# Halo copies issued by SyncE, the last minimum and maximum of a convolution moved behind a norm's sums, and a first pair of tiles normalised in halves

## Chip, cores and metric

The kernel runs on one core of a Trainium2 chip. The metric is the device time of one execution in microseconds; lower is better. An execution of the kernel before takes 2997.45 us (median of three, 2994.02 to 2998.33).

## What is computed

The input x has the shape (T, B, N, D) = (4, 8, 512, 512) in float32. Four layers follow each other, each of the form x = x + L(groupnorm(x)), with four groups of two channels for each t:

```
x = x + L0(gn(x))   # spiking attention block, by far the longest part
x = x + L1(gn(x))   # depthwise 13x13 Gaussian convolution, reflected edges
x = x + L2(gn(x))   # quantised 3x3 convolution, 8 channels to 8
x = x + L3(gn(x))   # 3x3 convolution with a bias

# L2:
sx  = 127 / max(abs(gn(x)))             # one maximum over the whole tensor
qx  = clip(round(gn(x) * sx), -127, 127)
out = conv3x3(qx, qw) / (sx * sw) + bias
```

Two things in this matter here. The scale of layer 2 needs the largest |gn(x)| of the whole tensor, so layer 2 can't start before layer 1 has given its last element. And the norm of layer 3 at time t needs all of layer 2's result of that t.

## The kernel before

Layer 0 ends a little after 2100 us and is not touched. Layer 1 and the fused layers 2 and 3 follow.

**Layer 1.** `Layer1.image` (from line 779) convolves one image on TensorE (PE, L797). For each half `a` of it, ScalarE evicts the result (L804), VectorE (DVE) takes its statistics (`bn_stats`, L806), its maximum `hi` (L807) and its minimum `lo` (L808), and DMAs on ScalarE's and GpSimd's queues (L815) write it to HBM. After the last image of a pair of channels, `next_norm` (from line 840) forms the group's mean and standard deviation: `group_stats` sums over the free axis on DVE (L175, `gsum_x`), sums over the partitions with a small matmul (L178, `gps_x`), squares the differences and sums again, and GpSimd (POOL) takes the power -0.5 (L195, `grstd_x`). `group_steps` is the same as a generator, which hands control back after the sums and after the matmul. From mean, deviation, `hi` and `lo` comes the largest |gn(x)| of the group (L854 to L858); `layers23` (from line 979) takes the maximum over the groups and partitions (L989 to L1001) and folds the scale into `r_own` and `mr_own` (L1009, L1010).

**Layers 2 and 3.** The rows of one t lie in tiles of 128 partitions (windows of rows times channels) by 512 columns. Two tiles make a pair, 22 pairs one t (N_PAIRS), the last with only half a tile. The loop at the end of `layers23` runs over n = 0 to 112. Each step has:

- a load of a pair (SyncE, L1033), five pairs ahead;
- `normalise`, two pairs ahead: two copies x to u on POOL that reorder columns (L1047), then y = u * r + mr on ScalarE (ACT, L1051, 128 x 1024 in one instruction);
- `quantise`, one pair ahead: xq, rounded to bfloat16, on DVE (L1062, 128 x 1024 in one instruction);
- `layer2`: three bfloat16 matmuls for each of the two tiles (L1080), and for each tile an instruction on DVE that adds u and writes layer 2's result into the ring x3 (L1087, called x in the profile), with its statistics by ACT (a square, L1093) or DVE (`bn_stats`, L1098);
- some halo copies (L1236). Layer 3 reads for each window also the row above and below, which lie in another window's partitions. `halos` gives the small copies within x3, from SBUF to SBUF. Every 11 pairs, from n = 14 on, a new list is made and worked off one or two copies per step. All in all there are 50 DMAs, issued by POOL;
- from n = 25 on `layer3` of pair n - 25: POOL writes the edge columns (L1175), 24 matmuls (L1182), two evictions o on ACT (L1191) and two stores on SyncE (L1198);
- behind the last pair of a t, `norm3`, a generator of which two steps run in each turn of the loop. It forms layer 3's norm (L1133 to L1164) and scales the weights `band_t` with it (L1151).

PSUM has three buffers for layer 2 and four for layer 3; u has four buffers, y two, o ten.

**What sets the order.** An engine works off its instructions in the order in which they stand in the program. That order is not wholly the one of the Python code: a planner lays it down when the program is built, from dependencies and estimated times. `tc.issue_after(op)` keeps an instruction behind another one: in each step `normalise` and `quantise` stand behind layer 2's instructions of the step before, and `layer2` behind these and behind layer 3 of the step before. On PE layer 2 and layer 3 alternate by pairs.

Of the kernel before, what the change touches and what calls it, by code (L numbers as in the profile page):

```python
# [37 lines left out]
AF = mybir.ActivationFunctionType  # L38
ALU = mybir.AluOpType
AX = mybir.AxisListType  # L40
# [3 lines left out]
T, B, N, D, H = 4, 8, 512, 512, 8  # L44
DH = D // H
NC = N // P
G = 4
# [3 lines left out]
ROUND = 12582912.0  # L51
# [9 lines left out]
N_PS1 = 4  # L61
# [65 lines left out]
def network(ctx: ExitStack, tc: tile.TileContext, i: dict, out: bass.AP):  # L127
    nc = tc.nc
# [3 lines left out]
    x2d = [tc.dram_tile([N * B, D], F32, name=f"x2_{t}") for t in range(T)]  # L132
# [7 lines left out]
    at = 0  # L140
# [102 lines left out]
    with ExitStack() as s:  # L243
        ps_1 = s.enter_context(pool("ps_2", space=PSUM))
        layer1 = Layer1(
            s, tc, x1d, x2d, avg, group_stats, r1, mr1, st2, m2, r2, most, w_sum, head, ps_1, pool
        )
        layer1.group(0)
        for g in range(1, G):
            if g == 1:  # L250
                with ExitStack() as behind:
                    for op in layer1.started:
                        behind.enter_context(tc.issue_after(op))
                    norm1(G - 1, ps_1)
                    w23 = weights23(tc, i, late, early["y"], ps_1, ident)
            layer1.group(g)
        layer1.next_norm(G - 1)
# [505 lines left out]

class Layer1:
    def __init__(
        self, s, tc, x1d, x2d, avg, group_stats, r1, mr1, st2, m2, r2, most, w_sum, head, ps_1, pool
    ):
        nc = tc.nc
        self.__dict__.update(
            nc=nc, x1d=x1d, x2d=x2d, avg=avg, group_stats=group_stats, r1=r1, mr1=mr1, st2=st2, m2=m2,  # L770
            r2=r2, most=most, ps_1=ps_1, w_sum=w_sum,
        )
        self.band, self.eye, *self.head = head
        self.ps_c = s.enter_context(pool("ps_c", 4, space=PSUM))
        self.xp = s.enter_context(pool("x1", 3))
        self.bp = s.enter_context(pool("bt1", 2))
        self.op = s.enter_context(pool("o1", 2))
        self.ends = {}

    def image(self, g, b, t, off):  # L780
        nc = self.nc
        n_half = W1_N // 2
        hi, lo = self.ends[g]
        if (b, t) == (0, 0):
            xt, bt = self.head
        else:
            xt = self.xp.tile([K1_P, W1_N, X1_U], F32, tag="x", name=f"x1_{b}_{t}")
            load_image(nc, xt, self.x1d[t][b])
            bt = self.bp.tile([K1_P, SHIFTS, M1], F32, tag="bt", name=f"bt_{b}_{t}")
            image_bands(nc, bt, self.band, b, self.r1[:, g, t : t + 1], self.eye)  # L790
        xo = self.op.tile([P, n_half // N_PS1, N_PS1 * NV], F32, tag="xo", name=f"xo1_{b}_{t}")
        for a in range(n_half // N_PS1):
            ps = self.ps_c.tile([P, N_PS1 * NV], F32, tag="conv", name="ps_conv1")
            for z in range(SHIFTS):
                for q in range(2):
                    w0 = q * n_half + a * N_PS1
                    mm = nc.tensor.matmul(  # L797
                        ps[q * M1 : (q + 1) * M1, :],
                        lhsT=bt[:, z, :],
                        rhs=xt[:, w0 : w0 + N_PS1, z : z + NV],  # L800
                        start=z == 0,
                        stop=z == SHIFTS - 1,
                    )
            nc.scalar.activation(xo[:, a, :], ps, AF.Identity, bias=off[:, t : t + 1])  # L804
            at = b % PAIR
            nc.vector.bn_stats(self.st2[:, t, b, a, :], xo[:, a, :])  # L806
            nc.vector.tensor_reduce(hi[:, t, at, a : a + 1], xo[:, a, :], AX.X, ALU.max)  # L807
            op = nc.vector.tensor_reduce(lo[:, t, at, a : a + 1], xo[:, a, :], AX.X, ALU.min)  # L808
        if (b, t) == (0, 0):
            self.started = mm.ins, op.ins  # L810
        dst = self.x2d[t]
        for q in range(2):
            for f in range(PH):
                engine = nc.gpsimd if f % 2 else nc.scalar
                engine.dma_start(  # L815
                    bass.AP(
                        dst.tensor, dst.offset + (q * n_half * W1_OUT * B + b) * D + f * NV,
                        [[B * D, W1_OUT], [W1_OUT * B * D, n_half], [1, NV]],
                    ),
                    xo[q * M1 + f : (q + 1) * M1 : PH, :, :].rearrange("p a (w v) -> p (a w) v", v=NV),  # L820
                )
# [18 lines left out]
    def next_norm(self, g):  # L840

        nc = self.nc
        n_a = W1_N // 2 // N_PS1
        m, r = self.group_stats(
            self.st2[:, :, g * PAIR : (g + 1) * PAIR].rearrange(
                "p t b k (h z) -> p t (b k h) z", z=3
            ),
            T, PAIR * n_a * 2, None, self.avg, self.ps_1, f"x2_{g}",
        )
        nc.vector.tensor_copy(self.m2[:, :, g], m)  # L850
        nc.vector.tensor_copy(self.r2[:, :, g], r)
        every = [P, T, PAIR * n_a]
        hi, lo = (x.rearrange("p t b a -> p t (b a)") for x in self.ends.pop(g))
        nc.vector.tensor_sub(hi, hi, m.unsqueeze(2).to_broadcast(every))  # L854
        nc.vector.tensor_sub(lo, m.unsqueeze(2).to_broadcast(every), lo)
        nc.vector.tensor_tensor(hi, hi, lo, op=ALU.max)
        nc.vector.tensor_mul(hi, hi, r.unsqueeze(2).to_broadcast(every))
        nc.vector.tensor_reduce(self.most[:, g : g + 1], hi, AX.XY, ALU.max)  # L858
# [118 lines left out]
def layers23(  # L977
# [47 lines left out]
    def load(t, p):  # L1025
# [3 lines left out]
        for a, q in first.items():  # L1029
# [8 lines left out]
                ),  # L1038
            )

    def normalise(t, p):
        n, n_p = len(tiles(p)), HALF * len(windows(tiles(p)[-1]))
        x = ahead.pop((t, p))[:n_p, :n, :]
        u = early["u"].tile([P, 2, D], F32, tag="u", name="u2")
        y = early["y"].tile([P, 2, D], F32, tag="y", name="y2")
        for j in range(n):
            nc.gpsimd.tensor_copy(  # L1047
                u[:n_p, j, :].rearrange("p (v g) -> p v g", g=PH),
                x[:, j, :].rearrange("p (g v) -> p v g", g=PH),
            )  # L1050
        op = nc.scalar.activation(  # L1051
            y[:n_p, :n, :], u[:n_p, :n, :], AF.Identity, bias=w["mr"][:n_p, t : t + 1],
            scale=w["r"][:n_p, t : t + 1],
        )
        ready[t, p] = u, y[:n_p, :n, :]
        return op.ins

    def quantise(t, p):
        u, y = ready[t, p]
        n_p, n, _ = y.shape  # L1060
        xq = w["xq"][(t * N_PAIRS + p) % 3]
        op = nc.vector.tensor_scalar(  # L1062
            xq[:n_p, :n, 2 : D + 2], y, ROUND, ROUND, op0=ALU.add, op1=ALU.subtract
        )
        ready[t, p] = u, xq
        return op.ins

# [142 lines left out]
    for n in range(n_all + N_PAIRS + LAG):  # L1210
        if n < n_all:
            for m in range(6) if n == 0 else [n + 5]:
                if m < n_all:
                    load(*divmod(m, N_PAIRS))


            with ExitStack() as order:
                for op in done.values():
                    order.enter_context(tc.issue_after(op))
                for m in range(3) if n == 0 else [n + 2]:  # L1220
                    if m < n_all:
                        first = normalise(*divmod(m, N_PAIRS))
                for m in range(2) if n == 0 else [n + 1]:
                    if m < n_all:
                        then = quantise(*divmod(m, N_PAIRS))
            with ExitStack() as order:
                for op in (first, then, *behind):
                    order.enter_context(tc.issue_after(op))
                did = layer2(*divmod(n, N_PAIRS))
        next(norm, None)  # L1230
        if n_chunk < n <= n_all + 3 and n % n_chunk == 3:
            t, p = divmod(n - 3 - n_chunk, N_PAIRS)
            copies = list(halos(t, p, p + n_chunk))
            at_once = -(-len(copies) // (n_chunk - 2))
        for _ in range(min(at_once, len(copies))):
            nc.gpsimd.dma_start(*copies.pop(0))  # L1236
        if n >= N_PAIRS + LAG:
            t, p = divmod(n - N_PAIRS - LAG, N_PAIRS)
            with tc.issue_after(did):
                behind = (layer3(t, p, *norms[t]),)  # L1240
        if n < n_all and n % N_PAIRS == N_PAIRS - 1:
            norm = norm3(n // N_PAIRS)
        next(norm, None)
# [36 lines left out]
```

## Time and profile before

The page describes one execution of 2991.6 us. An engine's share is its busy time over that span.

| Engine | busy us | share |
|---|---|---|
| PE (matmul) | 2900.4 | 97% |
| DVE | 2243.8 | 75% |
| POOL | 1035.6 | 35% |
| ACT | 550.0 | 18% |

The stages that the diff touches, from the trace:

| Stage | us from the start |
|---|---|
| layer 1's last matmul ends | 2560.94 |
| layer 2's first matmul | 2573.18 |
| layer 2 alone | 2573 to 2650 |
| first matmul of layer 3 | 2650.81 |
| layers 2 and 3 together | 2651 to about 2925 |
| layer 3 alone | to about 2984 |
| end, after the last eviction and store | 2991.6 |

In a timeline line the first number is the start in us, the second the duration, then engine, line, operation, output<-input with shapes, and the number of instructions taken together. Square brackets hold the engine's idle time before it and what ended that. In a row of a table by stage the stretch and its length come first, then busy us of PE, PE's weight loads, DVE, ACT and POOL with the number of instructions in brackets, then PE's granted clock, the DMA engines' share and GB/s.

In the group of lines for the halo copies, busy time stands first, then the mean of one in ns, then POOL's idle time before them with what ended it:

```profile
L1236 POOL DMA_DIRECT2D x<-x x50 | 30.8, 618 | 18.7 <-DVE sums L1136 12.0 <-issue 2.8 <-DMA out<-o 2.8
```

The 50 issues are busy for 30.8 us on POOL in all, 618 ns each.

### The profile page before, as it was taken

Reading aid. Unit: us, or ns where it says so; the run is one execution under the profiler, and the core shown is the slowest. Engines: PE = TensorE matmul, PEld = TensorE weight load, DVE = VectorE, ACT = ScalarE, POOL = GpSimd, SP = SyncE. Lnnn points to the kernel's source line nnn. Section 1 sums busy time; section 2 is a strip of 40 time slices with the busy share of each in tenths; the row PEclk is TensorE's granted clock in tenths of the full one; section 3 lists DMA queues with packets and bytes.
Section 4 is the critical chain, followed back from the end, with each engine's and each line's share of the span. In section 5 each row is a group of like instructions: output and inputs, shape, how many; then the busy total and the mean of one; then the engine's idle time right before and its main releaser. Section 6 shows DMA issues by size and latency. Waiting matters only on the chain. (4 is left out here: it accounts for less than half of the span.)

```text
span 2991.6 us, 37579 instructions
## 1 busy us (share of the span) xinstructions
PE 2900.4 (97%) x13343; PEld 1391.5 (47%) x13377; DVE 2243.8 (75%) x3883; ACT 550.0 (18%) x859; POOL 1035.6 (35%) x1928
## 2 busy tenths in 40 slices
PE   7999999999999999999999999999999999689999
PEld 3545555555555555555555555555333333223334
DVE  7887788788769868967986886786665566888880
ACT  2200010011010001001000100100111121676674
POOL 3332233333224333323432333341211112676650
PEclk9999999999999999999999999999999999889999
DMA  5312222222222221212221111111877778698865
GB/s 189 109 58 65 78 65 65 65 64 65 78 65 65 65 72 58 78 65 65 65 69 47 58 43 51 51 56 45 208 203 216 204 210 227 160 198 223 220 175 147
DMA packets 274651, 322.16 MB, mean 108 GB/s; under 512 B 21495, under 2 KB 171711, under 8 KB 274351
## 3 DMA queue, kind: packets, MB, share of 16 engines
q1 hardware_dynamic: 212304, 236.70, 29.3%
q0 software_dynamic: 20192, 56.83, 6.1%
q10 hardware_dynamic: 41967, 26.23, 3.0%
q8 instruction: 105, 1.72, 0.3%
q14 instruction: 83, 0.68, 0.1%
HBM read 210.57 MB, written 103.60 MB: 105 GB/s over the span
## 5 line engine op out<-in xcount | busy, mean ns | idle before, releaser
L485 PE MATMUL ps_in<-w_v,xn 128*128 128x512 f32 x1024 | 465.0, 603 | 2.6 <-DVE w_kq L344 2.6
L485 PE MATMUL ps_in<-xn,w_kq 128*128 128x512 f32 x1024 | 452.9, 595 | 5.1 <-DVE v_q L441 3.7
L485 PE MATMUL ps_in<-w_kq,xn 128*128 128x512 f32 x1024 | 449.8, 592 | 0.7 <-DVE v_k L450 0.7
L797 PE MATMUL ps_conv<-x,bt 112*64 112x512 f32 x2048 | 445.1, 592 | 0.1
L521 PE MATMUL ps_b<-toep,vtok 128*64 128x512 bf16 x3072 | 373.6, 383 | 0.0
L433 ACT ACTIVATE h_q<-v_q,c_half 128x512 f32<-128x512 f32 x96 | 69.3, 722 | 1550.6 <-DVE v_q L429 1164.1
L570 POOL COPY x1s<-x1s 128x2 f32<-128x2 f32 (+1 forms) x1024 | 227.4, 276 | 297.8 <-DVE x1s L559 297.8
L548 PE MATMUL ps_out<-wp,so 128*128 128x512 f32 x1024 | 308.5, 443 | 0.0
L458 POOL TENSOR_TENSOR h_v<-h_v,c_v 128x512 f32<-128x512 f32 x96 | 123.2, 1283 | 517.1 <-DVE h_v L457 505.4
L485 PEld LDWEIGHTS ps_in<-xn,w_kq 128*128 128x128 f32 x1024 | 191.9, 190 | 228.1 <-issue 212.4
L485 PEld LDWEIGHTS ps_in<-w_kq,xn 128*128 128x128 f32 x1024 | 194.2, 190 | 222.0 <-issue 205.2
L485 PEld LDWEIGHTS ps_in<-w_v,xn 128*128 128x128 f32 x1024 | 191.6, 192 | 216.9 <-issue 211.5
L797 PEld LDWEIGHTS ps_conv<-x,bt 112*64 112x64 f32 x2048 | 146.1, 135 | 288.4 <-issue 286.7
L521 PEld LDWEIGHTS <-vtok 128*64 128x64 bf16 x3072 | 207.6, 111 | 126.2 <-issue 4.9
L1182 PE MATMUL ps_conv<-x,band_t 64*64 64x512 f32 x2040 | 246.4, 599 | 3.1 <-DVE band_t L1151 3.1
L1047 POOL COPY u<-x 128x512 f32<-128x512 f32 (+1 forms) x172 | 208.7, 1247 | 95.8 <-issue 48.5
L548 PEld LDWEIGHTS ps_out<-wp,so 128*128 128x128 f32 x1024 | 192.5, 188 | 94.6 <-issue 57.8
L559 DVE SCALAR_TENSOR_TENSOR x1s<-v_p,xr 128x256 f32<-128x256 f32 x256 | 187.0, 770 | 14.9 <-DMA x<-x1s 3.9
L195 POOL TENSOR_TENSOR grstd_x<-grstd_x,neg_half 128x1 f32<-128x1 f32 (+1 forms) x28 | 20.9, 748 | 474.0 <-DVE grstd_x L194 474.0
L815 POOL DMA_DIRECT2D x<-xo x128 | 71.4, 565 | 312.5 <-ACT xo L804 298.2
L804 ACT ACTIVATE xo<-ps_conv,off 128x512 f32<-128x512 f32 x128 | 87.7, 687 | 430.6 <-PE ps_conv L797 316.0
L458 POOL TENSOR_TENSOR h_k<-h_k,c_k 128x512 f32<-128x512 f32 x96 | 122.8, 1279 | 116.4 <-DVE h_k L457 116.4
(191 smaller groups left out, 3557.8 us busy)
## 6 DMA issues: line engine op xcount, KB each, us to landing
x<-x SPq DMA_DIRECT2D x64, 917.0 KB
x<-x SPq DMA_DIRECT2D x168, 256.0 KB
x<-x1s POOLq DMA_DIRECT2D x128, 262.0 KB, 2.5
x<-in_x SPq DMA_DIRECT2D x128, 256.0 KB
xr<-in_x SPq DMA_DIRECT2D x128, 256.0 KB
out<-o SPq DMA_DIRECT2D x164, 192.0 KB
xs<-in_x SPq DMA_DIRECT2D x112, 256.0 KB
x<-xo ACTq DMA_DIRECT2D x128, 128.0 KB
```

The costliest lines, as they stand in the source:

```text
L433: nc.scalar.activation(h, v, AF.Identity, bias=c_col, scale=0.5)
L458: nc.gpsimd.tensor_add(h, h, c_twice[n])
L485: mm = nc.tensor.matmul(ps, lhsT=lhsT, rhs=rhs, start=k == 0, stop=k == NC - 1)
L521: nc.tensor.matmul(pb[two * DH : (two + 1) * DH, :], lhsT=v[:, c, h * DH : (h + 1) * DH], rhs=toep[z][:, h, u : u + N], start=c == 0 and z ...
L548: nc.tensor.matmul(ps, lhsT=so[:, k, c * P : (c + 1) * P], rhs=wpT[z][:, k, :], start=k == 0 and z == 0, stop=k == NC - 1 and z == 1,)
L559: nc.vector.scalar_tensor_tensor(own, v.rearrange("p (g v) -> p g v", g=PH)[:, two, :], 1.0, by_phase[:, two, :], op0=ALU.is_ge, op1=ALU.add,)
L570: nc.gpsimd.tensor_copy(x1[:, f, u : u + n], x1[:, fm, um - n + 1 : um + 1][:, ::-1])
L797: mm = nc.tensor.matmul(ps[q * M1 : (q + 1) * M1, :], lhsT=bt[:, z, :], rhs=xt[:, w0 : w0 + N_PS1, z : z + NV], start=z == 0, stop=z == SH ...
L804: nc.scalar.activation(xo[:, a, :], ps, AF.Identity, bias=off[:, t : t + 1])
L815: engine.dma_start(bass.AP(dst.tensor, dst.offset + (q * n_half * W1_OUT * B + b) * D + f * NV, [[B * D, W1_OUT], [W1_OUT * B * D, n_half] ...
L1047: nc.gpsimd.tensor_copy(u[:n_p, j, :].rearrange("p (v g) -> p v g", g=PH), x[:, j, :].rearrange("p (g v) -> p v g", g=PH),)
L1182: mm = nc.tensor.matmul(ps[j][b * HALF : (b + 1) * HALF, :], lhsT=band[half, b, dx, :], rhs=x3[half, s0 + j, dx : dx + D], start=dx == 0, ...
```

## The change

Three edits, for two places in which PE isn't full: the step from layer 1 to layer 2, and the stretch with layer 2 alone.

1. The halo copies are issued by SyncE instead of POOL. This takes them out of the queue in which the copies to u stand.
2. The maximum and the minimum of layer 1's very last tile are issued inside the norm's steps, behind the first sum, so that the norm's chain needn't wait for them. For that `Layer1` gets the generator `group_steps`.
3. The first pair of layer 2 (t = 0, p = 0) is normalised and quantised tile by tile, so that the first matmuls need only the first half.

```diff
@@ Layer1.image
             nc.vector.bn_stats(self.st2[:, t, b, a, :], xo[:, a, :])
-            nc.vector.tensor_reduce(hi[:, t, at, a : a + 1], xo[:, a, :], AX.X, ALU.max)
-            op = nc.vector.tensor_reduce(lo[:, t, at, a : a + 1], xo[:, a, :], AX.X, ALU.min)
+            for end, op in ((hi, ALU.max), (lo, ALU.min)):
+                args = end[:, t, at, a : a + 1], xo[:, a, :], AX.X, op
+                if (b, t, a) == (B - 1, T - 1, n_half // N_PS1 - 1):
+                    self.last_ends.append(args)
+                else:
+                    op = nc.vector.tensor_reduce(*args)
@@ Layer1.next_norm
-        m, r = self.group_stats(
+        steps = self.group_steps(
...
+        while True:
+            try:
+                next(steps)
+                if g == G - 1 and self.last_ends:
+                    nc.vector.tensor_reduce(*self.last_ends.pop(0))
+                next(steps)
+            except StopIteration as end:
+                m, r = end.value
+                break
@@ layers23
+    def tiles_apart(t, p, n):
+
+        return [slice(j, j + 1) for j in range(n)] if (t, p) == (0, 0) else [slice(0, n)]
@@ normalise
-        op = nc.scalar.activation(
-            y[:n_p, :n, :], u[:n_p, :n, :], AF.Identity, bias=w["mr"][:n_p, t : t + 1],
-            scale=w["r"][:n_p, t : t + 1],
-        )
+        for j in tiles_apart(t, p, n):
+            op = nc.scalar.activation(
+                y[:n_p, j, :], u[:n_p, j, :], AF.Identity, bias=w["mr"][:n_p, t : t + 1],
+                scale=w["r"][:n_p, t : t + 1],
+            )
@@ quantise
-        op = nc.vector.tensor_scalar(
-            xq[:n_p, :n, 2 : D + 2], y, ROUND, ROUND, op0=ALU.add, op1=ALU.subtract
-        )
+        for j in tiles_apart(t, p, n):
+            op = nc.vector.tensor_scalar(
+                xq[:n_p, j, 2 : D + 2], y[:, j, :], ROUND, ROUND, op0=ALU.add, op1=ALU.subtract
+            )
@@ the loop over n
         for _ in range(min(at_once, len(copies))):
-            nc.gpsimd.dma_start(*copies.pop(0))
+            nc.sync.dma_start(*copies.pop(0))
```

More of the change, by code (lines that the diff above doesn't have):

```diff
@@ L245, in network @@
         layer1 = Layer1(
-            s, tc, x1d, x2d, avg, group_stats, r1, mr1, st2, m2, r2, most, w_sum, head, ps_1, pool
+            s, tc, x1d, x2d, avg, group_steps, r1, mr1, st2, m2, r2, most, w_sum, head, ps_1, pool
         )
@@ L765, in __init__ @@
     def __init__(
-        self, s, tc, x1d, x2d, avg, group_stats, r1, mr1, st2, m2, r2, most, w_sum, head, ps_1, pool
+        self, s, tc, x1d, x2d, avg, group_steps, r1, mr1, st2, m2, r2, most, w_sum, head, ps_1, pool
     ):
@@ L769, in __init__ @@
         self.__dict__.update(
-            nc=nc, x1d=x1d, x2d=x2d, avg=avg, group_stats=group_stats, r1=r1, mr1=mr1, st2=st2, m2=m2,
+            nc=nc, x1d=x1d, x2d=x2d, avg=avg, group_steps=group_steps, r1=r1, mr1=mr1, st2=st2, m2=m2,
             r2=r2, most=most, ps_1=ps_1, w_sum=w_sum,
@@ L777, in __init__ @@
         self.op = s.enter_context(pool("o1", 2))
-        self.ends = {}
+        self.ends, self.last_ends = {}, []
     def image(self, g, b, t, off):
```

## The prediction

> **What bounds the kernel now.** I read the engine table first, then the slices, then a table by stage, then single instructions.
>
> ```profile
> PE 2900.4 (97%) x13343; PEld 1391.5 (47%) x13377; DVE 2243.8 (75%) x3883; ACT 550.0 (18%) x859; POOL 1035.6 (35%) x1928
> ...
> PE   7999999999999999999999999999999999689999
> ```
>
> PE is busy 97% of 2991.6 us. Only slices 35 and 36 (2543 to 2692 us) drop to 6 and 8; that is where the diff works. The table by stage (PE, PEld, DVE, ACT, POOL busy; clock; DMA):
>
> ```profile
> 2580.00:2590.00 10.00, 5.80 (x24) 2.21 (x23) 9.70 (x21) 10.00 (x20) 10.00 (x9) 1.00 0.80 201
> 2600.00:2620.00 20.00, 11.71 (x38) 4.33 (x39) 19.39 (x34) 16.82 (x33) 16.65 (x17) 0.86 0.94 164
> ...
> 2660.00:2680.00 20.00, 19.89 (x147) 6.40 (x142) 15.03 (x26) 15.17 (x26) 18.08 (x34) 1.00 1.02 239
> ```
>
> From 2573 to 2650 us there is only layer 2, and DVE sets the pace. From 2650.81, layer 3 runs too and PE does (19.89 of 20.00): 1.41 us of layer 2 and 2.73 of layer 3, 4.14 per pair. So a halo taken off POOL can pay only before 2650, and a late y or xq costs PE time only after it.
>
> **What the Trainium skill says.** "GPSIMD Engine Reference", section 1 Specifications: GpSimd shares its SBUF interfaces with VectorE and contends with it in the 2-port modes. The trace agrees: the same xq takes about 1.12 us beside a POOL copy, 3.38 beside a halo issue, and 0.68 beside an idle POOL:
>
> ```profile
> 2599.05 1.12 DVE L1062 TENSOR_SCALAR xq<-y 128x1024 bf16<-128x1024 f32 x1
> ...
> 2602.10 0.74 POOL L1236 DMA_DIRECT2D x<-x  x1
> ...
> 2604.14 3.38 DVE L1062 TENSOR_SCALAR xq<-y 128x1024 bf16<-128x1024 f32 x1
> ...
> 2608.97 2.47 POOL L1047 COPY u<-x 128x512 f32<-128x512 f32 x2 [2.02 <-issue]
> ...
> 2618.06 0.68 DVE L1062 TENSOR_SCALAR xq<-y 128x1024 bf16<-128x1024 f32 x1
> ```
>
> "DMA: Bandwidth & Descriptors", section SWDGE vs HWDGE vs iDMA: GpSimd writes its descriptors to rings in SBUF, and DMAs of Sync don't touch that path. No row here shows a halo on SyncE, but the long xq and POOL's 2.02 us of idle fit. "TensorE: Matmul & The Clock Gate", Part 1: after about 3.4 us of idleness the array runs at half clock (426.7 against 215.7 ns for 512 columns). The trace agrees: six layer-2 matmuls take 1.48 us, and 2.72 after some gaps.
>
> **The change, part by part.**
>
> *Last minimum behind the sums.* In the built order only `lo` moves; `hi` stays ahead.
>
> ```profile
> 2562.90 0.68 DVE L808 TENSOR_REDUCE lo<-xo 128x1 f32<-128x512 f32 x1
> 2563.49 0.23 DVE L175 TENSOR_REDUCE gsum_x<-st 128x4 f32<-128x64 f32 x1
> ```
>
> gsum_x can start 2563.49 − 2562.90 = 0.59 us earlier, and `lo` runs during PE's 0.59 us of gps_x. −0.6, or nothing if it delays gmean_x by as much.
>
> *First pair tile by tile.* y of the first pair takes 1.23 us and xq 0.69; by halves the first matmul needs 0.69 + about 0.40, some 0.8 less. DVE then waits for the rest, so I keep −0.4. Start in all −1.0 (−0.6 to −1.2).
>
> *Halos on SyncE, t = 0.* Three xq of pairs 13 to 21 carry an issue: 3.38, 3.30 and 2.30 us in place of 1.12. That is 2.26 + 2.18 + 1.18 = 5.6, of which POOL's lead absorbs some; by undisturbed pairs of 2.54 us, the norm's first instruction (2630.67) would come at about 2626.8: −3.8.
>
> *Later halos*: off POOL while PE is full: nothing, hidden behind PE's 19.89 of 20.00. *SyncE's queue*: an issue takes 0.65 us there (1.29 for two loads). Two loads, two halos and two stores are 3.9 at most in 4.14 us. A halo that waits for its x holds up the loads behind it by 1 to 3 us; these stand five pairs ahead, some 12 us even at 2.54 per pair. Nothing. Stores behind a halo have ten o buffers; landing took 6.4 us (median) from POOL and is needed some ten pairs later. Nothing.
>
> **What moves without a line in the diff.** The order on each engine is settled when the program is built, and taking the halos out of POOL's queue changed it elsewhere. I compared the built orders, with pair k counted from 0 to 87 and o(n) the layer-3 result of step n (pair n − 25).
>
> *Norm of t = 0*: it stands in one piece on DVE ahead of xq of pair 23, and POOL has the power and ten edges between two u. Before, L1133 to the first layer 3 took 2650.81 − 2630.67 = 20.1; walking the new order with the same durations gives 23: +2.9. *Norm of t = 1*: layer 2 of pair 44 to that of 48 took 22.8; new walk 21.0: −1.8. *t = 2*: 23.5, new walk 25.0: +1.5. These include y(46), y(67), y(69) of the next point.
>
> *ScalarE*, the main term. PE alternates layer 2 of k and layer 3 of step k. Before, y(k) mostly stands ahead of o(k − 4), three pairs of slack. After, in 11 places y(k) stands **behind o(k − 1)**: k = 33, 34, 46, 54, 55, 56, 67, 69, 76, 77, 78. ScalarE runs in order, so PE ends layer 3 of step k − 1, both o are evicted, then y(k), then xq(k), and only then can layer 2 of k start; layer 3 of step k is queued behind it. A steady pair shows the terms:
>
> ```profile
> 2717.61 2.81 PE L1182 MATMUL ps_conv<-x,band_t 64*64 64x512 f32 x24
> ...
> 2719.37 1.23 ACT L1051 ACTIVATE y<-u,mr_own,r_own 128x1024 f32<-128x1024 f32 x1
> ...
> 2720.35 1.47 PE L1080 MATMUL ps_conv<-xq,band 128*128 128x512 bf16 x6
> 2720.51 1.24 ACT L1191 ACTIVATE o<-ps_conv,const 128x512 f32<-128x512 f32 x2
> ```
>
> From PE's end of layer 3: 0.09 to o, 1.24 for two, y 1.23, 0.16 to xq, xq 0.69 (1.25 beside a POOL copy), 0.13 to PE: 3.5 us of idle PE (4.1 with the slow xq), where before it was 0 (2720.35 against 2720.42). I take 3.5: POOL's lead on u lets its copies be over by then. For k = 33 only one o is ahead: 2.9. Outside the norms there are eight places: 2.9 + 7 × 3.5 = +27.4. Where y stands behind o(k − 2), 17 places, the y ends at 2.56 and xq by 3.9 after PE's end, inside the 4.14 of the next pair: nothing.
>
> *Clock.* Such gaps may cool PE. After a gap of 2.16 us layer 3 once took 4.13 in place of 2.81, once 2.81. So 0 to 2 us for each of eight gaps (a cold layer 2 adds 1.2, a part of layer 3 more); I take 0.6: +5.
>
> **Sum**: −1.0 − 3.8 + 2.9 − 1.8 + 1.5 + 27.4 + 5 = +30.2. 2997.45 + 30 = 3027; I say **3026**.
>
> **Rivals.**
> - *Only what the diff means happens*: ScalarE's order costs nothing because o or y comes sooner than I read, and the norms only gain: −1.0 − 3.8 − 1.8 = −6.6, 2991. For it: the three long xq are real. Against it: an in-order queue leaves PE nothing else to run. 8%.
> - *No stalls, but norms as walked*: −1.0 − 3.8 + 2.9 − 1.8 + 1.5 = −2.2, 2995, no difference. 5%.
> - *Half the stalls*: the runs 54 to 56 and 76 to 78 may hide part of each other's cost when DVE and POOL have caught up, and the clock stays up: some +10, 3008. For it: DVE is busy only 41.9 of 50 us there. Against: PE has nothing to catch up with. 15%.
> - *Stalls with a cold clock each time*, slow xq: 27.4 + 8 × 0.6 + 8 × 1.2 = 41.8, less 2.2: +40, 3037. For it: gaps of 3.5 us exceed the page's window. Against: PE is full before and after. 17%.
> - The forecast, +20 to +35: 55%.
>
> **How the numbers follow.** The likeliest case gives 3026. The range is 3002 to 3040: it takes in the half and the cold case and leaves out the two rivals without stalls (13%) and some tails. Faster 0.08, same 0.06 (the second rival and a bit), slower 0.86.
>
> **What would show it.** ScalarE: waits of y for nothing but its place, each right after two o at k = 54 to 56 and 76 to 78; PE idle 3.5 us ahead of layer 2, released by DVE's xq, some eight times, at about 2690, 2790 and 2890 us; PE's busy share in those stretches falling by 3.5 us for each. The halo rows gone from POOL, no xq above 1.3 us between 2600 and 2630, and `lo` after gsum_x. If PE stays at 4.14 us per pair through those stretches, the ScalarE step is wrong; if gaps are there but six matmuls after them take 2.7 us, the clock term is too small; if loads come late in SyncE's queue (POOL waiting for DMA x ahead of u), the step that calls SyncE free is.

## The result, and the profile after

The changed kernel takes 3036.59 us (median of four, 3035.32 to 3037.55), the one before 2997.11 on the same chip (median of four): a ratio of 1.0133, with an interval of 1.0115 to 1.0151. It is 39.5 us slower. Timed once more, it gave 1.0144 (1.0127 to 1.0161).

The engine table and PE's slices of the profile after, whose span is 3035.0 us:

```profile
PE 2912.1 (96%) x13377; PEld 1395.2 (46%) x13377; DVE 2203.4 (73%) x3884; ACT 550.1 (18%) x860; POOL 998.4 (33%) x1878
...
PE   7999999999999999999999999999999998598889
```

PE did the same work, with 11.7 us more of busy time, and lost most of the rest to idleness: the full slices of the stretch with layers 2 and 3 have become 8s. DVE and POOL are busy for less than before (the halo issues are gone, and no xq is long between 2600 and 2630 us), so more work on them isn't the cause. The stage times say where the loss lies:

| Stage, us | before | after | difference |
|---|---|---|---|
| layer 1's last matmul to layer 2's first | 12.24 | 10.95 | -1.3 |
| to the first matmul of layer 3 | 77.63 | 76.56 | -1.1 |
| to the end of layer 2 | 267.89 | 316.10 | +48.2 |
| to the end of layer 3 | 67.91 | 69.11 | +1.2 |

(The rows add up to +47.0. The two profiled executions also differ by 3.6 us the other way ahead of all this, where neither kernel was changed, so they lie 43.4 us apart. The timed ones lie 39.5 us apart: the rows are of one execution each.) What the change was for is there, 2.4 us of it. Nearly all that was lost lies in the stretch where PE sets the pace. The waits of the profile after between 2640 and 2970 us (total, times, longest):

```profile
ACT o L1211 <- PE ps_conv L1202: 107.3, 44, 7.1
...
DVE xq L1082 <- ACT y L1070: 95.5, 23, 7.5
...
PE ps_conv L1100 <- DVE xq L1082: 37.4, 13, 4.1
```

Each line is one link of a ring: ACT waits for PE, DVE for ACT, PE for DVE. A ring of waits means that the three work one after the other. One turn of it in the timeline, for pair 55:

```profile
2793.74 1.26 ACT L1211 ACTIVATE o<-ps_conv,const 128x512 f32<-128x512 f32 x2 [6.81 <-PE ps_conv L1202]
...
2794.90 1.24 ACT L1070 ACTIVATE y<-u,mr_own,r_own 128x1024 f32<-128x1024 f32 x1
...
2796.17 0.69 DVE L1082 TENSOR_SCALAR xq<-y 128x1024 bf16<-128x1024 f32 x1 [6.42 <-ACT y L1070]
...
2796.91 1.56 PE L1100 MATMUL ps_conv<-xq,band 128*128 128x512 bf16 x6 [3.21 <-DVE xq L1082]
...
2798.40 4.35 PE L1202 MATMUL ps_conv<-x,band_t 64*64 64x512 f32 x24
```

Follow the numbers: ACT had been idle for 6.81 us and could have computed y long before, but o stood ahead of y and waited for PE. Then come two o, y, xq, and only then PE, idle for 3.21 us. The last line is the second loss: layer 3 takes 4.35 us in place of 2.81. PE has gaps released by xq at eleven places, for k = 33, 34, 46, 54, 55, 56, 67, 69, 76, 77 and 78.

### The profile page after: what moved, and what is told of

It is laid out like the page before. It is cut to its first block, busy times and chain, and to the rows that moved or that the text cites. A ratio compares the mean times of both kernels' runs of the same rounds, so it can differ in the third digit from the quotient of the medians.

```text
span 3035.0 us, 37632 instructions
## 1 busy us (share of the span) xinstructions
PE 2912.1 (96%) x13377; PEld 1395.2 (46%) x13377; DVE 2203.4 (73%) x3884; ACT 550.1 (18%) x860; POOL 998.4 (33%) x1878
## 5 line engine op out<-in xcount | busy, mean ns | idle before, releaser
L1065 POOL COPY u<-x 128x512 f32<-128x512 f32 (+1 forms) x172 | 201.5, 1209 | 172.6 <-DMA x<-x 60.5
L1202 PE MATMUL ps_conv<-x,band_t 64*64 64x512 f32 x2040 | 255.6, 617 | 0.0
L1100 PE MATMUL ps_conv<-xq,band 128*128 128x512 bf16 (+1 forms) x516 | 139.5, 409 | 67.8 <-DVE xq L1082 67.8
```

The lines of the kernel that those rows point to most:

```text
L1065: nc.gpsimd.tensor_copy(u[:n_p, j, :].rearrange("p (v g) -> p v g", g=PH), x[:, j, :].rearrange("p (g v) -> p v g", g=PH),)
L1100: mm = nc.tensor.matmul(ps[:n_p, :], lhsT=w["band2"][:n_p, j, dx, :n_p], rhs=xq[:n_p, j, dx + 1 : dx + 1 + D], start=dx == 0, stop=dx == 2,)
L1202: mm = nc.tensor.matmul(ps[j][b * HALF : (b + 1) * HALF, :], lhsT=band[half, b, dx, :], rhs=x3[half, s0 + j, dx : dx + D], start=dx == 0, ...
```

## The experiments

**1. Part 1 alone.**

```diff
 # the kernel before
-            nc.gpsimd.dma_start(*copies.pop(0))
+            nc.sync.dma_start(*copies.pop(0))
```

> Only part 1 of the change (halo copies issued by SyncE), parts 2 and 3 left out. The built order on ScalarE has the same eleven late y as the changed kernel. Order theory (PE idles because y(k) stands behind o(k-1) on ScalarE) and queue theory (halo copies in SyncE's queue hold up loads and stores): both about 3038 us, the changed kernel plus 1.3 us for the start. If parts 2 and 3 were what costs: about 2997.

Measured: 1.0137 (1.0120 to 1.0155), and 310.92 us from layer 3's first matmul to the end of layer 2. One word of the diff makes the whole loss. That doesn't tell yet whether by SyncE's queue or by the order.

**2. Parts 2 and 3 alone.**

```diff
 # the changed kernel
-            nc.sync.dma_start(*copies.pop(0))
+            nc.gpsimd.dma_start(*copies.pop(0))
```

> Only parts 2 and 3 (last minimum behind the sums, first pair in halves), halo copies issued by POOL as before. Order and queue theory: 1.3 us less than before, about 2995.8, and the stretch from layer 1's last matmul to layer 2's first 1.3 us shorter, 10.95 in place of 12.24. If the gain of the start comes from the freed POOL or is made up for later: 2997, no difference.

Measured: 1.0005 (0.9997 to 1.0012). The start is shorter in its trace (10.97 us in place of 12.24), but the time doesn't show it: 1.3 us would be 0.9996, just outside the interval. In the profiled execution the stretch with layers 2 and 3 took 271.62 us, 3.7 more than in the profile of before with the same order. 3.4 us of that are two places (at 2742.97 and 2841.76) where layer 3 stands behind a gap of 1.55 us on PE: its 22 matmuls took 4.49 us there, at half clock, and 2.79 behind the same two gaps in the kernel before. What takes up the 1.3 us in the timed executions isn't shown; so the gain of the start is shown as a stage and not as a time.

**3. The order on ScalarE put right, halo copies left on SyncE.**

```diff
 # the changed kernel; `first` is the latest y, of pair n + 2
-            with tc.issue_after(did):
+            with tc.issue_after(did), tc.issue_after(first):
                 behind = (layer3(t, p, *norms[t]),)
```

> The changed kernel, with one more order: o(n) on ScalarE stands behind y(n+2), so that no y is late. Halo copies stay in SyncE's queue, and DVE and POOL keep the changed order. Order theory: the eight gaps outside the norms vanish with their cold matmuls, some 8 x 4.4 = 35 us, and the ones at the norms in part: 2995 to 3003. Queue theory: the loads still come late, POOL goes on waiting for them, and the time stays above 3025.

Measured: 1.0000 (0.9992 to 1.0007), inside what was expected (2995 to 3003 us is 0.9993 to 1.0020); the stretch is back at 268.85 us. POOL's largest wait in that run, with total, times and longest (first line), and the stage rows of two stretches in which the changed kernel had its gaps:

```profile
POOL u L1065 <- DMA x<-x: 55.9, 35, 5.2
```

```profile
2680.00:2700.00 20.00, 19.79 (x144) 6.38 (x142) 16.97 (x30) 17.44 (x28) 16.08 (x14) 1.00 0.92 271
...
2790.00:2810.00 20.00, 19.89 (x146) 6.41 (x148) 12.97 (x25) 14.68 (x25) 9.24 (x9) 1.00 0.79 191
```

In the changed kernel the first of these rows reads:

```profile
2680.00:2700.00 20.00, 16.79 (x82) 5.03 (x85) 10.84 (x20) 9.94 (x15) 8.65 (x8) 0.69 0.51 148
```

PE is full again (19.79 against 16.79 of 20.00) although POOL still waits 55.9 us for loads, where it waited 3.1 us in the kernel before. So POOL does wait for loads once the halo copies stand in SyncE's queue, and that costs next to nothing, since the copies to u are early enough. The queue theory falls.

**4. The order alone, in the kernel before.**

```diff
 # the kernel before; LATE = (33, 34, 54, 55, 56, 76, 77, 78)
+        if n + 1 in LATE:                      # at the end of step n, behind layer3
+            with ExitStack() as order:
+                order.enter_context(tc.issue_after(last_o[0]))
...
+                first = scaled_y(*divmod(n + 1, N_PAIRS))
+                then = quantise(*divmod(n + 1, N_PAIRS))
```

(At their usual place in the step these eight y and xq are left out.)

> The kernel before with halo copies on POOL, and y(k) put behind o(k-1) by hand for k = 33, 34, 54, 55, 56, 76, 77 and 78, nothing else. Order theory: eight gaps of 3.2 to 4.1 us on PE ahead of layer 2, each followed by matmuls at half clock in part, 8 x 4.4 = +35: about 3032 (3024 to 3036). Queue theory: nothing is in SyncE's queue that wasn't there, about 2997.

Measured: 1.0124 (1.0109 to 1.0139), that is +37 us, as expected, without any halo copy on SyncE. PE's idle time shows at the eight chosen pairs and is 3.21 to 3.24 us each time; two of them:

```profile
2692.97 1.46 PE L1086 MATMUL ps_conv<-xq,band 128*128 128x512 bf16 x6 [3.22 <-DVE xq L1068]
...
2794.71 2.72 PE L1086 MATMUL ps_conv<-xq,band 128*128 128x512 bf16 x6 [3.22 <-DVE xq L1068]
```

Same gap, and once the six matmuls take 1.46 us, once 2.72. Experiments 3 and 4 together settle the cause: the late y is enough to lose the time, and without it the loss is gone.

**5 and 6. The half clock after the gaps.** Twelve extra matmuls fill most of each of eight gaps:

```diff
 # the changed kernel; WARM = (33, 34, 54, 55, 56, 76, 77, 78)
+        if n + 1 in WARM:
+            with tc.issue_after(behind[0]):
...
+                for i in range(12):
+                    mm = nc.tensor.matmul(ps, lhsT=w["band2"][:, 0, 0, :], rhs=flat[:, :D], ...)
+                behind = (mm.ins,)
```

> The changed kernel, with twelve extra bfloat16 matmuls of 128x512 on constant weights (result unused) on PE between layer 3 of step k-1 and layer 2 of pair k, for k = 33, 34, 54, 55, 56, 76, 77, 78. They fill about 12 x 0.213 = 2.6 us of each gap of 3.2 us, so the gap itself costs the same. If the matmuls at half clock after the gaps (13 us in the changed kernel's trace at these eight places, 1.6 us each) come from the idleness, they go: about 3037 - 13 = 3024. If the clock falls for another reason, or the half clock is only a mark of the gaps: 3037 or more.

> The changed kernel once more, side by side with the one with filled gaps on the same chip. Ratio to before 1.013 as measured.

> The changed kernel with twelve extra matmuls in eight of its gaps, side by side with the changed kernel. If the half clock after the gaps costs in the timed executions what it cost in the one that was profiled (13 us in the eight places): 10 to 13 us less than the changed kernel, ratio to before about 1.009 to 1.010. If the timed executions mostly keep their clock, or the extra matmuls cost elsewhere what they save: no difference, 1.013.

In the trace it is clear. Layer 3, the filling, and the next layer 2 and layer 3 around pair 34:

```profile
2684.51 2.81 PE L1203 MATMUL ps_conv<-x,band_t 64*64 64x512 f32 x24
...
2687.25 2.76 PE L1267 MATMUL ps_warm<-band 128*128 128x512 bf16 x12
...
2690.53 1.47 PE L1101 MATMUL ps_conv<-xq,band 128*128 128x512 bf16 x6 [0.51 <-DVE xq L1083]
...
2691.93 2.81 PE L1203 MATMUL ps_conv<-x,band_t 64*64 64x512 f32 x24
```

Layer 2 still starts 3.2 us after layer 3's end (2687.32 to 2690.53), but all eight places run at 1.47 and 2.81 us, and the stretch is 305.63 us in the one profile and 307.56 in the other, 10.6 less than the 316.10 and 318.28 of the changed kernel. So in the traces the half clock comes from the idleness. The times don't show it clear of noise. The first timing gave 1.0136 (1.0120 to 1.0152), where my 3024 us would be 1.009 and the rival had 3037 or more; side by side with the changed kernel it was 1.0125 (1.0110 to 1.0140) against 1.0144 (1.0127 to 1.0161), nearer to "no difference" than to my 1.009 to 1.010. The intervals overlap; the means of eight runs each, over both timings, are 3031.0 and 3036.8 us. My 13 us were too much for a typical execution. The profiled executions overstate it: the one of the changed kernel in the second timing was the slowest of its four (3044.07 us), the two with filled gaps were the fastest of theirs (3029.99 and 3026.10). The cost by place varies as well: I add up what layers 2 and 3 take over 1.40 and 2.81 us at the eight places, and find 6.5 us in experiment 1, 13.1 and 14.9 in the two profiles of the changed kernel.

**7. A version that beats both.** As experiment 3, and the norm's steps behind the latest xq:

```diff
 # the kernel of experiment 3, at both places where the norm goes on
-        next(norm, None)
+        with tc.issue_after(then):
+            next(norm, None)
```

> The changed kernel with o(n) behind y(n+2) on ScalarE, and the steps of layer 3's norm on DVE behind the latest xq, so that no xq of the next pairs stands behind a whole norm. Halo copies stay on SyncE. Order theory: all of the intended gain appears: start -1.3, layer 2 of t = 0 by 4.3 shorter, its norm back from 23.4 to about 20, the gaps of 6.98, 3.75 and 2.53 us at the norms gone: 6 to 9 us below the kernel before, ratio 0.997 to 0.998. Rival (a norm that ends later delays layer 3 by as much as xq gains, or SyncE's queue still costs something): within 0.1% of before.

Measured: 0.9972 (0.9961 to 0.9983), that is 8.4 us below the kernel before. Layer 2's first matmul to layer 3's first is 70.87 us (77.63 before), the following stretch 267.82. With both orders pinned, the change does what it was meant for: layer 2's last addition for t = 0 on DVE ends 56.1 us after its first matmul (60.3 before), 4.2 of the 6.8 us. The rest lies in the norm behind it. Whether the norm's pin would give that with the halo copies still on POOL was not run. The kernel isn't free of gaps: of 6.98, 3.75 and 2.53 us at the norms in experiment 3, gaps of 3.27, 1.82 and 1.31 are left, each behind a long xq like those of the next experiment.

**8. What makes an xq long.** In the changed kernel no halo copy is on POOL, and yet:

```profile
2630.69 6.03 POOL L1065 COPY u<-x 128x512 f32<-128x512 f32 x6
...
2634.03 3.25 DVE L1082 TENSOR_SCALAR xq<-y 128x1024 bf16<-128x1024 f32 x1 [3.46 <-ACT y L1070]
```

The six copies end at 2636.72, xq at 2637.28, 0.56 us later. So do the three long xq that the kernel before has between 2600 and 2630 us (0.57, 0.56 and 0.56 us after the last copy of a run). To separate the halo's issue from the run of copies, the kernel of experiment 7 got small POOL copies in its place:

```diff
 # the kernel of experiment 7
+            if n < N_PAIRS:
...
+                for _ in range(2):
+                    nc.gpsimd.tensor_copy(stand_in, last_x[0])    # 8x160
```

> The kernel with y first and the norm behind xq, halo copies on SyncE, and small copies of 8x160 on POOL (two for each of the five halo copies of t = 0) where a halo issue might have stood. No DMA is issued by POOL there. If an xq of 2.3 to 3.4 us comes from POOL's copies to u running without a break once something has put POOL behind (in the traces so far such an xq ends 0.56 us after the last copy of a run, with or without a halo): xq of over 2 us come back near pairs 17 to 20, and the time from layer 2's first matmul to the norm's first instruction grows by 1 to 4 us. If it comes from the DMA issue itself (descriptors that POOL writes): no xq above 1.6 us there, and no more than the 1 to 2 us that the small copies take on POOL.

Measured in the trace: 59.7 us from layer 2's first matmul to the norm's first instruction, against 56.1 in experiment 7, and the long xq are back without a halo on POOL:

```profile
2612.72 3.27 DVE L1082 TENSOR_SCALAR xq<-y 128x1024 bf16<-128x1024 f32 x1
...
2620.74 5.11 POOL L1065 COPY u<-x 128x512 f32<-128x512 f32 x5
...
2624.13 2.28 DVE L1082 TENSOR_SCALAR xq<-y 128x1024 bf16<-128x1024 f32 x1 [2.55 <-ACT y L1070]
```

The copies of the second end at 2625.85, the xq at 2626.41, again 0.56 us later. These are single executions, one of each kernel.

## Why the prediction was right, and where it was off

The forecast was 3026 us, some 29 above the kernel before; measured are 39.5. The main term held. Two terms were too small in the profiled executions, the half clock by 8 us and the norms of t = 1 and t = 2 by 8.6.

- **The late y, main term: right.** The eight gaps outside the norms are 3.30, 3.21, 4.09, 3.21, 3.21, 3.31, 3.24 and 3.23 us, 26.8 in all, where the sum had 27.4. Experiments 3 and 4 show the cause. For k = 33 the term of 2.9 was too small: one o fewer stood ahead, but its xq took 1.37 us beside a POOL copy. The 17 places with y behind o(k - 2) cost nothing, as said: there is no gap above 0.5 us at any of them outside the norms.
- **The clock: mechanism right, size wrong.** The term was 0.6 us for each gap, +5. The trace has 13.1 us at the eight places, 1.6 each: layer 2 up to 2.65 us to layer 3's start in place of 1.40, and layer 3 up to 4.36 in place of 2.81. I had taken the mean of two layer-3 runs after gaps of 2.16 us, which are shorter. The case with a cold clock each time (3037) came nearest to 3036.6, in part by luck: it added 4.8 us for slow xq, where the gaps come to 26.8 in all, and kept the norms of t = 1 and t = 2 at -0.3, where they cost 8.3.
- **The norms of t = 1 and t = 2: wrong.** The walks gave 21.0 and 25.0 us; measured from pair 44 to 48 and from 66 to 70 are 25.6 and 29.0, so +2.8 and +5.5 in place of -1.8 and +1.5. The walks put no half clock behind the gaps at k = 46, 67 and 69; layer 3 after k = 46 alone took 5.38 us. Over 1.40 and 2.81 us the half clock adds 4.9 us around k = 46 and 3.1 around 67 and 69; the walks fell short by 4.6 and 4.0 us. With the norms the stretch adds up: 26.8 + 13.1 + 2.8 + 5.5 = 48.2 us.
- **Start and t = 0: right.** -1.3 for -1.0. In the timeline `lo` starts at 2559.46, behind gsum_x at 2559.32, and `hi` stays ahead of it (2558.73); the first xq takes 0.43 us. Layer 2's first matmul to the norm's first instruction takes 53.2 us in place of 57.5, -4.3 for -3.8; from there to layer 3's first matmul 23.4 us for 23.
- **What makes xq long: effect right, cause wrong.** I put it down to the halo's issue, with the Trainium skill's note on descriptors in SBUF ("DMA: Bandwidth & Descriptors", section SWDGE vs HWDGE vs iDMA). Experiment 8 shows that it isn't needed: it is enough that something puts POOL behind, so that several copies then follow each other at about 1.05 us each. The prediction's own lines spoke against the issue: it ran from 2602.10 to 2602.84, and the long xq began only at 2604.14. The xq that did run beside it, in the kernel before, took 1.11 us:

```profile
2601.59 1.11 DVE L1062 TENSOR_SCALAR xq<-y 128x1024 bf16<-128x1024 f32 x1
```

- **SyncE's queue: right on the cost, wrong on the loads.** I had them five pairs early. They are often just in time, and POOL waits for them; but POOL has time to spare there. The 3.9 us that I summed for a step were too low: in the trace after, a halo's issue takes 0.75 us on SyncE and a store's 0.81 (medians), so two loads, two halos and two stores come to some 4.4 us, more than the 4.14 of a pair.
- The last stage grew by 1.2 us, of which I had said nothing. It did in the other two profiled kernels with SyncE's halo copies and the late y as well (69.1 to 69.4 us), and by half as much or less in those with y put first (68.1 to 68.6). In the former, 0.80 us of it is a wait of PE for gsum_x, a step of the last norm on DVE (at 2964.34 in the changed kernel), which the others don't have. The cause of the rest stays open.

## What to carry to other kernels

Moving one instruction to another queue can move the rest: here the planner, seeing a freed engine, laid down other orders on engines that the diff doesn't name, so compare the built orders engine by engine before believing in a gain. On an in-order engine look for a producer for the next step that stands behind a consumer of the last one; it closes a ring in which three engines take turns, and each turn costs the whole latency (here some 3.2 us), however idle these engines are on average. Pin the orders that matter by hand: here two were enough for 8.4 us less than the kernel before, with the rest left to the planner.

## What the hardware showed that I had not expected

- A DVE instruction with one SBUF input can wait for several instructions of POOL, not one. The Trainium skill, "SBUF — State Buffer", section Who interferes with whom, says of VectorE's 2-port modes that whoever issues first has the shared ports for the whole instruction and the other blocks. That xq runs in such a mode no run here shows. The runs agree that it blocks, but the xq of 3.25 us began inside a run of copies of about 1.0 us each and got through only after the last one, 0.56 us later, and so in the other traces. In the steady stretch (2590 to 2600 us in the kernel before) xq (1.1 us) also ends 0.56 us after a copy, but after the very copy in which it began; the next copy then takes 1.57 us in place of 1.05.
- A gap of 3.2 us is enough for the half clock, but not always. In the profile of experiment 1 four of the eight gaps left PE at full speed, in that of the changed kernel two. "TensorE: Matmul & The Clock Gate", Part 1, speaks of a free-running window of about 3.4 us. The traces agree: from 2590 to 2965 us PE's granted clock changes only on a grid of 3.41 us, at 2678.70, 2685.53, 2688.94 and 2695.77 in the changed kernel for instance. So what counts is how a gap lies on that grid. The two gaps of 3.22 us shown in experiment 4, with PE's busy time and clock in stretches of the grid:

```profile
2688.01:2691.42 3.41, 1.74 (x16) 1.00 0.61 155
2691.42:2694.84 3.42, 1.87 (x10) 1.00 0.81 152
...
2790.41:2793.82 3.41, 1.09 (x12) 1.00 0.52 135
2793.82:2797.24 3.42, 2.53 (x6) 0.50 0.87 234
```

The first gap (2689.75 to 2692.97) is split between two stretches, and the clock stays up. The second (2791.49 to 2794.71) lies mostly in one, and the next stretch is granted half. Over the eleven traces, from 2590 to 2965 us, each of the 58 full-clock stretches in which PE was busy for at most 1.32 us was followed by half clock, none of the 903 with over 2.14 us, and 11 of the 96 between. The page's cold state follows an idle window of about 3.4 us, and the prediction took it so; here a window only partly idle is enough, and the measurement decides.
